# Twelve opening steps of a causal attention, issued among the units of the feed-forward before it

## The chip, the cores and the metric

The kernel runs on one core of a Trainium2 chip. The metric is the device time of one execution in microseconds (us). The engines are TensorE (PE for its matmuls, PEld for its weight loads), VectorE (DVE), ScalarE (ACT), GpSimd (POOL) and SyncE (SP, which here only issues DMAs).

## The reference

Two layers work on x of 8 images x 512 tokens x 256 features in fp32. Layer 0 is a full 16-head attention plus a mixture of 8 experts. Layer 1, to which the change belongs, adds two things to x, both computed from its layernorm `xn`:

```python
qkv = xn @ Wqkv_w.T + Wqkv_b                 # 16 heads of 16
ctx = causal_attn(q, k, v)                   # softmax of q.k / 4 under a causal mask
q2  = conv1d(ctx, conv_w, 3 taps) + conv_b   # new queries
ctx2 = causal_attn(q2, k, v)                 # the same keys and values
attn = ctx2 @ out_w.T + out_b
...
H   = gelu((xn @ U1) @ V1 + b1)              # rank 64, 1024 hidden
ffn = (H @ U2) @ V2 + b2
x   = x + attn + ffn
```

## The kernel before

Everything for one image (512 tokens) fits on the 128 partitions, features or tokens across. The order of instructions on every engine is the order in which the program issues them; each engine takes its own in that order, and waits on the others by semaphores.

**The feed-forward** of layer 1 is a loop over 32 pairs of hidden chunks: 8 images (`b`) x 4 pairs (`c2`). Its units: `ffn_in` (L981) multiplies an image by U1 and DVE copies the result to `pT` (L986); `ffn_hidden` (L993) makes two hidden chunks at once, each on 64 of the array's rows, and ACT takes the gelu (L999); `ffn_rank` (L1006) sums the two chunks over U2, on 64 columns each, into bank 7; `ffn_out` (L1018) first has DVE copy the rank-64 result to `fqT` (L1013), then multiplies by V2 in two halves, each added by DVE into `acc` (L1022). Pair `n` issues, in this order: `ffn_in` of the next image (if `c2` is 1), the pieces of `second` due there, the hidden chunks of pair `n + 1`, the rank of pair `n`, and `ffn_out` (if `c2` is 3). `second` carries out the list `THIRD` beside pairs 0 to 20: gathers of expert results (`g`), their sums (`+`, `P`, L525), statistics, norms (`n`, `N`, on ACT, L260), and the transposition of images 4 to 7 to features (`f`, L269: two halves, copied out by DVE, L271, and by ACT, L273).

**The banks.** PSUM has eight banks that one list of names shares out. `bank(kind)` hands out the banks of a kind in turn. In the feed-forward, `hidden` has banks 0 to 3, `mm` has 4 to 6 and bank 7 holds the rank's sum.

**Layer 1's attention** is a list of 64 jobs: first attentions (`key` 1) for 8 images x 4 groups of four heads, and the second ones (`key` 2) seven places behind them in the list. A job has six steps of maxima and, 12 steps later (`LEAD[1]`), six steps of exponentials. `run` counts steps `t` over all jobs: at step `t` it issues the maxima of job `t // 6` (`scores`, L348) and the exponentials of job `(t - 12) // 6` (`exps`, L397, a mask matmul, L415, and ACT's Exp, L424), with the matmuls of both interleaved; then one task from a list with due times (`todo1`); then the attention matmuls due (`attend`, L437, from five steps after a job's first exponentials). A maxima step is two heads, each on 32 of the array's rows, over 512, 128 + 384 or 256 keys, and DVE reduces each part (L368). So in steps 0 to 11 there are maxima alone. What the list gives to these steps: projections of queries and keys for jobs 0 and 1 ahead of step 0 (`project`, L296, taken out by DVE, L286, for queries and by ACT, L288, for keys); values of image 0 at steps 1 and 2 (L306, L314); the transposition of job 0's maxima at step 6 (`shift`, L378, copied by L381, and four DMAs, L385, that put them into a spare row of the queries); projections for jobs 2 and 3 at steps 7 and 8. The kind `mx` (maxima) has three banks there, `sc` (exponentials) three, `av` one, `mm` one.

**The pools.** The pool `l1` (mask, value buffer, exponentials `e`, the convolution's input `ctxT`, `cT`) and `q1` (queries, keys) are opened behind the feed-forward, when the pools `mid` (its weights) and `ffn` are closed. POOL's adds of the output biases to `acc` (L1164) are issued while the list of jobs is built, that is ahead of step 0, one for each image.

Of the kernel before, what the change touches and what calls it, by code (L numbers as in the profile page):

```python
# [152 lines left out]
def block_kernel(ctx: ExitStack, tc: tile.TileContext, x, a0_wqk, a0_bqk, a0_wv, a0_bv, cent, experts,  # L153
# [168 lines left out]
    class Job:  # L322
# [64 lines left out]
        def exps(self, i):  # L387
            blocks, pr = SC_SEQ[self.seq][i]
            heads = [bank("sc") for _ in range(2)]
            parts, at = [], 0  # L390
            for kc in blocks:
                lo = kc * P if self.causal else 0
                parts.append((kc, at, lo))
                at += S - lo
            mm = [
                [
                    lambda h=h, kc=kc, at=at, lo=lo: nc.tensor.matmul(  # L397
                        heads[h % 2][:, at : at + S - lo],
                        lhsT=self.k[h * PH : (h + 1) * PH, kc * P : (kc + 1) * P],
                        rhs=self.q[h * PH : (h + 1) * PH, lo:],  # L400
                        start=kc == blocks[-1],
                        stop=not self.causal,
                    )
                    for h in (2 * pr, 2 * pr + 1)
                ]
                for kc, at, lo in reversed(parts)
            ]
            n = at

            def after():  # L410
                if self.causal:


                    for h in range(2):
                        nc.tensor.matmul(  # L415
                            heads[h][:, : len(blocks) * P], lhsT=ident_bf, rhs=mask_t[:, : len(blocks) * P],
                            start=False, stop=True,
                        )
                e = self.pool.tile(
                    [P, 2, n], F32, tag=f"e{blocks[0]}" if self.causal else "e", name=f"e{self.nm}_{i}",  # L420
                    bufs=3 if self.causal else 4,
                )
# [20 lines left out]
                )  # L443

    def run(jobs, work_of, layer, per_step, most):
        steps, lead = STEPS[layer], LEAD[layer]
        end = steps * len(jobs)
        if layer == 1:
# [120 lines left out]
    with ExitStack() as l0:  # L569
# [347 lines left out]
        jobs = []  # L917
        for b in range(NB):
            for g in range(HG):
                job = Job(f"0_{b}_{g}", False, 1.0, vbuf[b % 2], g, l0_done, q0)  # L920
                job.b = b
                jobs.append(job)

# [50 lines left out]
    cb_sb = load([P, 2, 2], conv_b, "cb_sb")  # L974
    ow_sb = load([P, 2, D], out_w, "ow_sb")

    with tc.tile_pool(name="ffn", bufs=1, side="right", reuse_waits="tile") as ffn:
        def ffn_in(b):
            ps = bank()
            for k in range(2):  # L980
                nc.tensor.matmul(  # L981
                    ps, lhsT=u1_sb[:, k, :, :].rearrange("p i r -> p (i r)"), rhs=xT1[b][:, k, :],
                    start=(k == 0), stop=(k == 1),
                )
            pT = ffn.tile([P, S], F32, tag="pT", name=f"pT{b}", bufs=2)
            nc.vector.tensor_copy(pT, ps)  # L986
            return pT

        def ffn_hidden(b, c2, pT):
            ps = [bank("hidden") for _ in range(2)]  # L990
            for i in range(2):
                fc, r = 2 * c2 + i, slice(i * RANK, (i + 1) * RANK)
                nc.tensor.matmul(  # L993
                    ps[i], lhsT=v1_sb[r, fc * P : (fc + 1) * P], rhs=pT[r, :], start=True, stop=True
                )
            hT = ffn.tile([P, 2, S], F32, tag="hT", name=f"gT{b}_{c2}", bufs=3)
            for i in range(2):
                fc = 2 * c2 + i
                nc.scalar.activation(  # L999
                    hT[:, i, :], ps[i], AF.Gelu_apprx_tanh, bias=fb1_sb[:, fc : fc + 1]  # L1000
                )
            return hT

        def ffn_rank(pq, c2, hT):
            for i in range(2):
                nc.tensor.matmul(  # L1006
                    pq[i * RANK : (i + 1) * RANK, :], lhsT=u2_sb[:, 2 * c2 + i, :], rhs=hT[:, i, :],
                    start=(c2 == 0), stop=(c2 == NFC // 2 - 1),
                )

        def ffn_out(b, pq):
            qT = ffn.tile([P, S], F32, tag="qT", name=f"fqT{b}", bufs=2)
            nc.vector.tensor_copy(qT, pq)  # L1013
            for h in range(2):
                ps = bank()
                for j in range(2):
                    c = 2 * h + j
                    nc.tensor.matmul(  # L1018
                        ps[:, j * D : (j + 1) * D], lhsT=qT[:, c * P : (c + 1) * P], rhs=v2_sb, start=True, stop=True
                    )  # L1020
                a = acc[b][:, 2 * h : 2 * h + 2, :].rearrange("p c d -> p (c d)")
                nc.vector.tensor_tensor(a, a, ps, ALU.add)  # L1022

        share_banks(hidden=banks[:4], mm=banks[4:7])
        late = iter(THIRD)
        pTs = {0: ffn_in(0)}
        ahead = [(0, 0, ffn_hidden(0, 0, pTs[0]))]
        pairs = [(b, c2) for b in range(NB) for c2 in range(NFC // 2)]
        pq = None
        out_of = None  # L1030
        for n, (b, c2) in enumerate(pairs):
            if c2 == 1 and b + 1 < NB:
                pTs[b + 1] = ffn_in(b + 1)
            second(next(late, ""))
            if n + 1 < len(pairs):
                nb, nc2 = pairs[n + 1]
                ahead.append((nb, nc2, ffn_hidden(nb, nc2, pTs[nb])))
            _, _, hT = ahead.pop(0)
            if c2 == 0:
                pq = banks[7]  # L1040
            ffn_rank(pq, c2, hT)
            if c2 == NFC // 2 - 1:
                ffn_out(b, pq)
# [6 lines left out]
    for i in range(2):  # L1050
        t = l1.tile([P, 2, S + 2], F32, tag=f"ctxT{i}", name=f"ctxT{i}", bufs=1)
        nc.gpsimd.memset(t[:, :, 0:1], 0.0)
        nc.gpsimd.memset(t[:, :, S + 1 : S + 2], 0.0)
        ctxT.append(t)

    cmask = l1.tile([P, S], F32, name="cmask", bufs=1)
    nc.gpsimd.memset(cmask, 0.0)
# [59 lines left out]
    def l1_done(job, t):  # L1117
# [13 lines left out]
        cT = l1.tile([P, 2, S], F32, tag="cT", name=f"cT{b}", bufs=1)  # L1131
# [24 lines left out]
        for h in range(2):  # L1156
            todo1.add(t + 6, t + 12 + h, 1.75, lambda h=h: project_out(h))

    firsts, seconds, jobs = [], [], []
# [124 lines left out]
```

## Time and profile before

| | us |
|---|---|
| median of three timed runs | 2101.22 |
| lowest, highest | 2099.24, 2106.05 |
| the profiled execution | 2090.77 |
| its span, first to last instruction | 2089.0 |
| feed-forward, first matmul to last | 987.9 to 1102 |
| steps 0 to 11 | 1102 to 1140 |
| granted PE clock, mean over the span | 0.983 |

The rows of the profile give times in microseconds from the span's start. "x4" counts instructions: an fp32 matmul is two of them. A number in square brackets in the timeline is the time in which the engine had nothing to do before the row, with what ended it. "issue" is time in which an engine waited for nothing that the profile shows. The granted clock is a share of full speed.

### The profile page before, as it was taken

The numbers are of one execution on the slowest core, as the hardware profiler recorded it, in microseconds if no ns is written. First come the engines' busy times: TensorE is split into PE (matmuls) and PEld (weight loads), VectorE is DVE, ScalarE is ACT, GpSimd is POOL, SyncE is SP. The second block draws the span as 40 slices with busy tenths as digits, with TensorE's granted clock in tenths as the row PEclk, the third lists the DMA queues.
The fourth block names the chain that finished last, engine by engine and source line by source line (L and its number), as shares of the span: only waits on it lengthen the run. The fifth ranks groups of instructions, "written<-read, shape, count | busy, mean of one in ns | idle before, by whom it ended". The sixth has DMA issues, their size and how long they took to land.

```text
span 2089.0 us, 35592 instructions
## 1 busy us (share of the span) xinstructions
PE 2005.6 (96%) x13672; PEld 1019.1 (49%) x13672; DVE 1229.8 (59%) x3565; ACT 867.3 (42%) x1690; POOL 203.0 (10%) x245
## 2 busy tenths in 40 slices
PE   5899999999999999998898999999999999999998
PEld 3334555555555455542334455555555545554554
DVE  5765554555455554565425666666666666666763
ACT  4443333333333333336541444444444444444444
POOL 4361010010110100013310000000000000000000
PEclk8899999999999999999997999999999999999999
DMA  9025132222322223102000000000000000000000
GB/s 330 24 65 184 59 116 83 93 80 96 117 79 97 74 102 114 67 26 79 21 0 1 2 2 2 2 12 2 2 13 2 12 2 12 2 12 2 2 12 21
DMA packets 46057, 105.60 MB, mean 51 GB/s; under 512 B 5952, under 2 KB 33984, under 8 KB 42944
## 3 DMA queue, kind: packets, MB, share of 16 engines
q0 software_dynamic: 6384, 59.78, 7.7%
q1 hardware_dynamic: 38656, 42.62, 6.1%
q8 instruction: 107, 1.75, 0.4%
q10 hardware_dynamic: 848, 0.93, 0.1%
q14 instruction: 62, 0.51, 0.1%
HBM read 76.05 MB, written 26.48 MB: 49 GB/s over the span
## 4 chain that ended last, share of the span: by engine, by line
PE 88%; DVE 6%; ACT 2%; issue 2%; DMA 1%; SPq 0%; POOL 0%; ACTq 0%; DVEq 0%; POOLq 0%
PE bank L348 30%; PE bank L437 13%; PE bank L810 8%; PE bank L831 8%; PE bank L296 5%; PE bank L415 4%; PE bank L1088 4%; PE bank L397 3%; PE bank L306 3%; DVE m L365 2%; PE bank L1106 2%; PE bank L993 1%; PE bank L1140 1%; PE bank L269 1%; PE bank L1006 1%
## 5 line engine op out<-in xcount | busy, mean ns | idle before, releaser
L424 ACT ACTIVATE e<-bank 128x512 f32<-128x512 f32 (+1 forms) x1280 | 638.8, 552 | 923.0 <-PE bank L397 464.6
L348 PE MATMUL bank<-k,q 32*128 32x512 f32 (+3 forms) x3072 | 759.3, 534 | 22.3 <-DVE m L365 18.4
L397 PE MATMUL bank<-q,k 32*128 32x512 f32 (+3 forms) x3072 | 689.4, 533 | 4.2 <-DMA q<-mT 3.4
L368 DVE CUSTOM_DVE_ANT_0 jk<-bank,cmask 128x512 bf16<-128x512 f32 (+3 forms) x1024 | 502.8, 491 | 241.5 <-PE bank L348 162.2
L348 PEld LDWEIGHTS bank<-k,q 32*128 32x128 f32 x3072 | 301.1, 187 | 381.5 <-issue 158.6
L365 DVE TENSOR_REDUCE m<-bank 128x1 f32<-128x512 f32 x512 | 328.9, 685 | 142.6 <-PE bank L397 112.1
L437 PE MATMUL bank<-e,v 128*32 128x512 f32 (+3 forms) x3072 | 318.8, 503 | 0.0
L397 PEld LDWEIGHTS bank<-q,k 32*128 32x128 f32 x3072 | 272.0, 186 | 17.6 <-issue 9.9
L810 PE MATMUL bank<-hsT,w 128*128 128x256 f32 x736 | 179.7, 389 | 1.3 <-DVE hsT L793 1.3
L831 PE MATMUL bank<-w,hT 128*128 128x256 f32 x736 | 169.2, 383 | 0.0
L810 PEld LDWEIGHTS bank<-hsT,w 128*128 128x128 f32 x736 | 133.5, 190 | 69.7 <-issue 52.8
L831 PEld LDWEIGHTS bank<-w,hT 128*128 128x128 f32 x736 | 136.5, 190 | 37.3 <-issue 20.9
L437 PEld LDWEIGHTS bank<-e,v 128*32 128x32 f32 x3072 | 67.8, 109 | 137.3 <-issue 132.3
L415 PE MATMUL bank<-mask_t,ident_bf 128*128 128x128 bf16 (+1 forms) x768 | 123.6, 245 | 0.0
L415 PEld LDWEIGHTS <-ident_bf 128*128 128x128 bf16 x768 | 44.1, 98 | 155.4 <-issue 140.4
L823 DVE TENSOR_SCALAR hT<-bank,w 128x256 f32<-128x256 f32 x92 | 44.5, 484 | 110.4 <-ACT hT L821 110.4
L1088 PE MATMUL bank<-ctxT,cw_sb 128*128 128x256 f32 x384 | 90.0, 384 | 2.1 <-DVE q L286 1.8
L368 DVE DVE_READ_ACCUMULATOR2_ANT m<- 128x1 f32 x1024 | 84.9, 83 | 0.1
L840 DVE TENSOR_TENSOR f<-bank,w 128x256 f32<-128x256 f32 x46 | 19.5, 425 | 102.8 <-PE bank L831 102.8
L821 ACT ACTIVATE hT<-bank,w 128x256 f32<-128x256 f32 x92 | 43.6, 474 | 79.8 <-PE bank L810 79.8
L1088 PEld LDWEIGHTS bank<-ctxT,cw_sb 128*128 128x128 f32 x384 | 70.2, 190 | 13.1 <-DVE q L286 3.2
L288 ACT ACTIVATE k<-bank,bqk,rows 128x512 f32<-128x512 f32 x64 | 46.3, 773 | 69.8 <-PE bank L296 60.4
(187 smaller groups left out, 1409.7 us busy)
## 6 DMA issues: line engine op xcount, KB each, us to landing
hs_d<-zeros SPq DMA_DIRECT2D x2, 5888.0 KB
hs<-hs_d SPq DMA_DIRECT2D x46, 256.0 KB
q<-mT SPq DMA_DIRECT2D x384, 2.0 KB
fs_d<-f SPq DMA_DIRECT2D x23, 256.0 KB
acc<-in_x SPq DMA_DIRECT2D x8, 512.0 KB
out<-acc SPq DMA_DIRECT2D x8, 512.0 KB
cw_sb<-in_conv_w SPq DMA_DIRECT2D x1, 768.0 KB
wqk<-in_a_wqk ACTq DMA_DIRECT2D x1, 512.0 KB
```

The lines of the kernel that those rows point to most:

```text
L296: nc.tensor.matmul(ps, lhsT=w[:, k, col : col + P], rhs=src[:, k, :], start=(k == 0), stop=(k == 1))
L306: nc.tensor.matmul(ps[:, j * D : (j + 1) * D], lhsT=src[:, k, c * P : (c + 1) * P], rhs=w[:, k, :], start=(k == 0), stop=(k == 1),)
L348: lambda h=h, qc=qc, at=at, nk=nk: nc.tensor.matmul(heads[h % 2][:, at : at + nk], lhsT=self.q[h * PH : (h + 1) * PH, qc * P : (qc + 1) * ...
L365: nc.vector.tensor_reduce(self.m[:, qc, h, :], src, AX.X, ALU.max, negate=True)
L368: nc.vector.tensor_tensor_reduce(out=junk[:, :nk], in0=src, in1=cmask[:, S - nk :], scale=1.0, scalar=-3e38, op0=ALU.add, op1=ALU.max, acc ...
L397: lambda h=h, kc=kc, at=at, lo=lo: nc.tensor.matmul(heads[h % 2][:, at : at + S - lo], lhsT=self.k[h * PH : (h + 1) * PH, kc * P : (kc + 1 ...
L415: nc.tensor.matmul(heads[h][:, : len(blocks) * P], lhsT=ident_bf, rhs=mask_t[:, : len(blocks) * P], start=False, stop=True,)
L424: nc.scalar.activation(e[:, h, :], heads[h][:, :n], AF.Exp, scale=self.scale)
L437: nc.tensor.matmul(self.av[h * PH : (h + 1) * PH, lo:], lhsT=self.v[:, kc, 4 * self.g + h, :], rhs=es[h // 2][:, h % 2, :], start=first, s ...
L810: nc.tensor.matmul(ps[:, i * TB : (i + 1) * TB], lhsT=w[:, O_W1 + k * FF + fc * P : O_W1 + k * FF + (fc + 1) * P], rhs=self.hsT[:, k, :], ...
L831: nc.tensor.matmul(ps[:, 0:D], lhsT=self.hT[:, fc, j * P : (j + 1) * P], rhs=w[:, O_W2 + fc * D : O_W2 + (fc + 1) * D], start=(fc == 0), s ...
L1088: nc.tensor.matmul(ps[:, :w], lhsT=cw_sb[:, k, tap, c * P : (c + 1) * P], rhs=ctxT[b % 2][:, k, tap + lo : tap + lo + w], start=(k == 0 an ...
```

## The change

The function `run` becomes a generator that yields after every step. It is made ahead of the feed-forward, and the feed-forward's loop asks it for one step after pairs 8, 10, 12, ... 30, so that steps 0 to 11 are issued there; the rest of the steps follow behind the loop. For this, the pools `l1` and `q1` are opened before the feed-forward, and a new pool `e1` for what is only needed from step 12 on (exponentials, `ctxT`, `cT`) is opened after it. In the feed-forward the kind `mm` has bank 4 alone, and the maxima have banks 5 and 6. The mask and the third value buffer are filled ahead of the feed-forward, and POOL's adds of the output biases come behind it.

```diff
     def run(jobs, work_of, layer, per_step, most):
...
             work_of.fill(t, per_step, most)
             attend(t)
+            yield t
         work_of.drain()
...
-        run(jobs, todo, 0, MOE_PER_STEP, 99)
+        for _ in run(jobs, todo, 0, MOE_PER_STEP, 99):
+            pass
...
-    mids.close()
-    banks_causal()
     l1 = ctx.enter_context(tc.tile_pool(name="l1", bufs=2, reuse_waits="tile"))
     q1 = ctx.enter_context(tc.tile_pool(name="q1", bufs=5, reuse_waits="tile"))
...
     def l1_job(key, n):
         b, g = divmod(n, HG)
-        if key == 1 and g == 0:
-            nc.gpsimd.tensor_tensor(acc[b], acc[b], ob_sb.unsqueeze(1).to_broadcast([P, NC, D]), ALU.add)
-        job = Job(f"{key}_{b}_{g}", True, 0.25, vbuf[b % 3], g, l1_done, l1)
+        job = Job(f"{key}_{b}_{g}", True, 0.25, vbuf[b % 3], g, l1_done, ep)
...
-    run(jobs, todo1, 1, 99.0, 1)
+
+    steps = run(jobs, todo1, 1, 99.0, 1)
+    with tc.tile_pool(name="ffn", bufs=1, side="right", reuse_waits="tile") as ffn:
...
-        share_banks(hidden=banks[:4], mm=banks[4:7])
+        share_banks(hidden=banks[:4], mm=banks[4:5], mx=banks[5:7])
...
             if c2 == NFC // 2 - 1:
                 ffn_out(b, pq)
+            if n >= len(pairs) - 2 * LEAD[1] and n % 2 == 0:
+                next(steps)
+
+    mids.close()
+    ep.append(ctx.enter_context(tc.tile_pool(name="e1", bufs=3, reuse_waits="tile")))
+    for i in range(2):
+        t = ep[0].tile([P, 2, S + 2], F32, tag=f"ctxT{i}", name=f"ctxT{i}", bufs=1)
+        nc.gpsimd.memset(t[:, :, 0:1], 0.0)
+        nc.gpsimd.memset(t[:, :, S + 1 : S + 2], 0.0)
+        ctxT.append(t)
+    banks_causal()
+    for b in range(NB):
+        nc.gpsimd.tensor_tensor(acc[b], acc[b], ob_sb.unsqueeze(1).to_broadcast([P, NC, D]), ALU.add)
+    for _ in steps:
+        pass
```

The feed-forward's functions are otherwise as they were, moved below the list of jobs.

More of the change, by code (lines that the diff above doesn't have):

```diff
@@ L418, in after @@
                         )
-                e = self.pool.tile(
+                e = self.pool[-1].tile(
                     [P, 2, n], F32, tag=f"e{blocks[0]}" if self.causal else "e", name=f"e{self.nm}_{i}",
@@ L919, in block_kernel @@
             for g in range(HG):
-                job = Job(f"0_{b}_{g}", False, 1.0, vbuf[b % 2], g, l0_done, q0)
+                job = Job(f"0_{b}_{g}", False, 1.0, vbuf[b % 2], g, l0_done, [q0])
                 job.b = b
@@ L975, in block_kernel @@
     ow_sb = load([P, 2, D], out_w, "ow_sb")
[L977 to L1022, printed above, removed]
-        share_banks(hidden=banks[:4], mm=banks[4:7])
[L1025 to L1043, printed above, removed]
@@ L1049, in block_kernel @@
     ctxT = []
[L1050 to L1054, printed above, removed]
     cmask = l1.tile([P, S], F32, name="cmask", bufs=1)
@@ L1130, in l1_done @@
             return
-        cT = l1.tile([P, 2, S], F32, tag="cT", name=f"cT{b}", bufs=1)
+        cT = ep[0].tile([P, 2, S], F32, tag="cT", name=f"cT{b}", bufs=1)
         for k in range(2):
@@ L1157, in l1_done @@
             todo1.add(t + 6, t + 12 + h, 1.75, lambda h=h: project_out(h))
-    firsts, seconds, jobs = [], [], []
+    firsts, seconds, jobs, ep = [], [], [], []
     def l1_job(key, n):
         b, g = divmod(n, HG)
-        if key == 1 and g == 0:
-            nc.gpsimd.tensor_tensor(acc[b], acc[b], ob_sb.unsqueeze(1).to_broadcast([P, NC, D]), ALU.add)
-        job = Job(f"{key}_{b}_{g}", True, 0.25, vbuf[b % 3], g, l1_done, l1)
+        job = Job(f"{key}_{b}_{g}", True, 0.25, vbuf[b % 3], g, l1_done, ep)
         job.b, job.key = b, key
@@ L1194, in block_kernel, with ffn_in, ffn_hidden, ffn_rank @@
             l1_job(2, n - LAG)
-    run(jobs, todo1, 1, 99.0, 1)
+    steps = run(jobs, todo1, 1, 99.0, 1)
+    with tc.tile_pool(name="ffn", bufs=1, side="right", reuse_waits="tile") as ffn:
+        def ffn_in(b):
+            ps = bank()
+            for k in range(2):
+                nc.tensor.matmul(
+                    ps, lhsT=u1_sb[:, k, :, :].rearrange("p i r -> p (i r)"), rhs=xT1[b][:, k, :],
+                    start=(k == 0), stop=(k == 1),
+                )
+            pT = ffn.tile([P, S], F32, tag="pT", name=f"pT{b}", bufs=2)
+            nc.vector.tensor_copy(pT, ps)
+            return pT
+        def ffn_hidden(b, c2, pT):
+            ps = [bank("hidden") for _ in range(2)]
+            for i in range(2):
+                fc, r = 2 * c2 + i, slice(i * RANK, (i + 1) * RANK)
+                nc.tensor.matmul(
+                    ps[i], lhsT=v1_sb[r, fc * P : (fc + 1) * P], rhs=pT[r, :], start=True, stop=True
+                )
+            hT = ffn.tile([P, 2, S], F32, tag="hT", name=f"gT{b}_{c2}", bufs=3)
+            for i in range(2):
+                fc = 2 * c2 + i
+                nc.scalar.activation(
+                    hT[:, i, :], ps[i], AF.Gelu_apprx_tanh, bias=fb1_sb[:, fc : fc + 1]
+                )
+            return hT
+        def ffn_rank(pq, c2, hT):
+            for i in range(2):
+                nc.tensor.matmul(
+                    pq[i * RANK : (i + 1) * RANK, :], lhsT=u2_sb[:, 2 * c2 + i, :], rhs=hT[:, i, :],
+                    start=(c2 == 0), stop=(c2 == NFC // 2 - 1),
+                )
+        def ffn_out(b, pq):
+            qT = ffn.tile([P, S], F32, tag="qT", name=f"fqT{b}", bufs=2)
+            nc.vector.tensor_copy(qT, pq)
+            for h in range(2):
+                ps = bank()
+                for j in range(2):
+                    c = 2 * h + j
+                    nc.tensor.matmul(
+                        ps[:, j * D : (j + 1) * D], lhsT=qT[:, c * P : (c + 1) * P], rhs=v2_sb, start=True, stop=True
+                    )
+                a = acc[b][:, 2 * h : 2 * h + 2, :].rearrange("p c d -> p (c d)")
+                nc.vector.tensor_tensor(a, a, ps, ALU.add)
+        share_banks(hidden=banks[:4], mm=banks[4:5], mx=banks[5:7])
+        late = iter(THIRD)
+        pTs = {0: ffn_in(0)}
+        ahead = [(0, 0, ffn_hidden(0, 0, pTs[0]))]
+        pairs = [(b, c2) for b in range(NB) for c2 in range(NFC // 2)]
+        pq = None
+        out_of = None
+        for n, (b, c2) in enumerate(pairs):
+            if c2 == 1 and b + 1 < NB:
+                pTs[b + 1] = ffn_in(b + 1)
+            second(next(late, ""))
+            if n + 1 < len(pairs):
+                nb, nc2 = pairs[n + 1]
+                ahead.append((nb, nc2, ffn_hidden(nb, nc2, pTs[nb])))
+            _, _, hT = ahead.pop(0)
+            if c2 == 0:
+                pq = banks[7]
+            ffn_rank(pq, c2, hT)
+            if c2 == NFC // 2 - 1:
+                ffn_out(b, pq)
+            if n >= len(pairs) - 2 * LEAD[1] and n % 2 == 0:
+                next(steps)
@@ new lines, in block_kernel @@
+    mids.close()
+    ep.append(ctx.enter_context(tc.tile_pool(name="e1", bufs=3, reuse_waits="tile")))
+    for i in range(2):
+        t = ep[0].tile([P, 2, S + 2], F32, tag=f"ctxT{i}", name=f"ctxT{i}", bufs=1)
[7 more added lines that the diff above has]
+        pass
```

## The prediction

> **What bounds the kernel now.** I read the page first, then the chain of waits around the feed-forward, then windows by stage, then the timeline where a bank is reused. The page says TensorE (PE) is the bound, and that its clock is granted in full except around 1100 to 1150 us.
>
> ```profile
> PE 2005.6 (96%) x13672; PEld 1019.1 (49%) x13672; DVE 1229.8 (59%) x3565; ACT 867.3 (42%) x1690; POOL 203.0 (10%) x245
> ...
> PEclk8899999999999999999997999999999999999999
> ```
>
> The chain shows the feed-forward as almost pure PE work, and then the twelve steps.
>
> ```profile
> 1080.83 1.91 PE bank L981 x4
> 1082.74 1.06 PE bank L993 x4
> 1083.80 1.01 PE bank L1006 x4
> ...
> 1089.02 0.70 DVE fqT L1013
> 1089.72 0.04 issue
> 1089.77 2.00 PE bank L1018 x8
> ...
> 1118.10 1.11 PE bank L348 x4
> 1119.20 0.67 DVE jk L368
> ...
> 1133.20 1.98 PE bank L296 x4
> ```
>
> One pair of the feed-forward is hidden 1.06 plus rank 1.01; an image adds ffn_in 1.91 and ffn_out 0.74 (a DVE copy PE waits for) plus 2.00: 13.0 us, all PE. A step is 1.11 of maxima (0.56 for the 256-key ones), sometimes a projection (1.98) or values (1.98), with waits for DVE between.
>
> ```profile
> 1017.40:1102.10 84.70, 77.77 (x297) 29.37 (x298) 20.66 (x35) 41.77 (x69) 14.13 (x6) 1.00 0.00 0
> 1102.10:1140.10 38.00, 33.10 (x99) 15.56 (x97) 20.47 (x71) 4.17 (x5) 2.34 (x1) 0.80 0.00 1
> 1140.10:1158.10 18.00, 18.00 (x86) 9.24 (x85) 9.02 (x37) 5.66 (x12) 0.00 (x0) 0.50 0.01 2
> ...
> 1118.35:1121.76 3.41, 2.98 (x14) 1.24 (x10) 2.76 (x10) 0.00 (x0) 0.00 (x0) 1.00 0.00 0
> ...
> 1312.90:1316.31 3.41, 3.41 (x28) 2.21 (x28) 2.67 (x11) 2.12 (x4) 0.00 (x0) 1.00 0.02 5
> ```
>
> The columns are window, length, busy PE, PEld, DVE, ACT, POOL, then granted clock. The feed-forward from image 2 on (first row) keeps PE busy for 77.8 of 84.7 us: there is little room. The twelve steps (second row) take 38.0 us at a mean clock of 0.80, and steps 12 to 17 (third row) run wholly at half clock.
>
> **The clock, from the rows.** It changes on a grid of 3.41 us. I weigh PE's busy time by the share of the array's row strips in use: maxima alone use two of four. The window 1118.35 to 1121.76 has 2.98/2/3.41 = 0.44, and the next ones run at 0.50; windows at 0.41 (1108.11) and 0.44 (1135.41) did the same. Windows with a dense projection and a gap, 1.98/3.41 = 0.58 (1104.69), stayed at 1.00. So the edge lies between 0.44 and 0.58. Four strips at once at full clock keep it (the 1312.90 row); at half clock they did not win it back in six windows, until the first attention matmul (L437) at 1156.3.
>
> The Trainium skill, "TensorE: Matmul & The Clock Gate", section "Why this matters for your kernels", asks only that PE not idle for some 3 us between matmuls; by it alone nothing here would slow down, and no window of the changed feed-forward either. The 1118.35 row, busy for 2.98 of 3.41 us, differs, and I go by the row.
>
> **What is removed.** The 38.0 us between the end of ffn_out at 1102.05 and step 12 at 1140.05.
>
> **What the feed-forward gains.** Steps 0 to 11 follow pairs 8, 10, ... 30 on PE, in order. PE work: maxima 2 jobs x 2 x (1.11 + 1.11 + 0.56) = 11.1; four projections 7.9; two values 4.0; one transpose 0.3: 23.3 us. PE idles only 2.6 us there that this can fill, at images 2 and 3 (16.45 and 15.1 us against 13.0 plus 0.87 of transposes), where it waits for ACT's norms: -2.6.
>
> **The bank.** The feed-forward's other matmuls rotate over banks 4 to 6; now bank 4 alone serves them and the steps' tasks, as 5 and 6 hold maxima. Each reuse waits for the copy out. Its price is in these rows:
>
> ```profile
> 1089.77 2.00 PE L1018 MATMUL bank<-v_sb,fqT 128*128 128x256 f32 x8 [0.82 <-DVE fqT L1013]
> 1090.93 0.69 DVE L1022 TENSOR_TENSOR acc<-acc,bank 128x512 f32<-128x512 f32 x1 [1.22 <-PE bank L1018]
> ...
> 1105.55 1.98 PE L296 MATMUL bank<-yT,wqk 128*128 128x512 f32 x4 [1.62 <-DVE q L286]
> ```
>
> The first half of ffn_out ends at 1090.77, DVE's add ends at 1091.62, and PE follows 0.05 later: 0.90 us, in which everything behind it on PE waits too.
> - ffn_out's second half: 8 x 0.9 = 7.2.
> - The four transposed images (pairs 11, 14, 17, 20): second half after the first's copy, 4 x 0.9 = 3.6; and before the first half 0.9 to 1.0 after values (pair 11), ffn_in (17) and ffn_out (20): 2.9.
> - ffn_in after values (pair 13) 1.0, after the transposed maxima (pair 21; DVE has 1.55 of maxima queued first, then 0.27) 1.8, after a k projection (pair 25; ACT's two takes, 1.45) 1.65: 4.4.
> - Step 0: k's projection after q's 1.62, maxima after the first k take 0.92: 2.5, as before the change.
>
> Sum 20.6. The lower bound is step 0's 2.5 alone; I take 20.6, since each wait has its row and PE issues in order. The feed-forward grows by 23.3 - 2.6 + 20.6 = 41.3, against 38.0 removed: **+3.3**.
>
> The Trainium skill, "Perfetto Trace Analysis", section "Optimizing Tensor Performance", speaks against this edit: independent matmul groups should rotate through PSUM banks so that copying one out overlaps the next group's matmuls. By it the waits come in full, without it only step 0's remain, and the growth would be 23.2; the 1.62 us row sides with it.
>
> **The clock after.** Step 12 now follows dense pairs. Steps 12 to 17 at full clock are bound by DVE: three such steps take 5.0 us (its maxima rows run from 1312.53 to 1317.55), so 10.1 for six, 0.3 for a copied transpose, 1.0 for L437: 11.4, against 18.1 before (1140.05 to 1158.14); and 1.2 us more that ran at half clock shrink to 0.6: **-7.3**. Bounds: 0 if the clock falls anyway; -9.6 if DVE bounded nothing and all 19.3 us halved. But the waits thin some windows: at pair 21 half of 1.11, 0.3, then 1.8 of nothing and 0.35 of ffn_in is 1.2/3.41 = 0.35, below the edge for about two thirds of the grid's phases. At pair 20, 0.9 idle, 1.0, 0.9 idle, 0.44 and 0.17 idle make 1.44/3.41 = 0.42, and pairs 14 and 17 come to about the same, in a fifth of the phases each. One fallen window costs half of 3.41: **+1.7** (bounds 0 to 4 x 1.7).
>
> **Covered edits.** The eight POOL adds (2.35 us each, L1164) move from within the feed-forward to behind it, 19 us of POOL beside steps 12 on; acc is next needed by L1147 about 240 us later. The mask and value memsets (2.9 us) move ahead of the last gathers, where POOL idles 8.9 us; uncovered they cost 2.9. The moved transpose's four DMAs leave on SP some 45 us before step 12 reads them. DVE's maxima (1.0 to 2.15 us) stand ahead of fqT's copy, behind 2.07 us of PE: at most 0.1. ACT's Exp table load (1.28) falls under the last ffn_out (3.6). The e tiles' new pool waits only for ffn_out's own reads.
>
> **Sum:** 3.3 - 7.3 + 1.7 = -2.3 us. The profiled execution's 2090.8 (span 2089.0, 1.8 around it) becomes 2088.5; it lies 10.4 below the median of the timed runs, 2101.2, which goes to 2098.9. Its own range, with no to three fallen windows and 5 us either way on the waits, is 2092 to 2106.
>
> **Rivals.**
> - *The waits cost half.* PEld loads the next weights during a wait, and some waits may meet ones already there (ACT's norms at images 2 and 3, the 0.74 before ffn_out). Growth 23.3 - 2.6 + 10.3 = 31.0; -38.0 - 7.3 gives -14, 2087. For it: PE has hidden work on other banks queued close behind. Against: it is queued behind, not ahead.
> - *The clock is lost at the seam (slower).* If a window near the last ffn_out (0.74 and 0.9 idle of 3.6) or of steps 12 to 14, DVE-bound, falls under the edge, it stays at half until L437, since four strips did not lift it in six windows. Then -7.3 is gone, and with three fallen windows (5.1): 3.3 + 5.1 = +8.4, 2110. It decides once that share is below 0.44 to 0.58. Against: the 1312.90 row.
> - *Neither clock nor wait differs much*: the stretch merely changes place, within 2 us.
>
> **How the numbers follow.** The forecast has 0.52, the cheap waits 0.26, the lost clock 0.20, the last 0.02. A measurement of this kernel tells about 0.3% (6.3 us) from no change. The forecast's fast quarter (no window falls, waits over-counted by 2.3 us or more) is beyond that: 0.15. Faster 0.15 + 0.26 = 0.41; same 0.37 + 0.02 = 0.39; slower 0.20. The range runs from a cheap-waits case to near the lost clock: 2086 to 2109.
>
> **What would show it.** Right: step 12 near 1145 (1102.05 + 41.3 + 1.7); L1018 waiting 0.9 for L1022 eight times; clock 1.00 in the 12 us behind it; L437 some 11 us after step 12. Wrong: growth under 33 us (waits oversized), or clock 0.50 behind step 12 (the seam), or fallen windows in most images.

## The result, and the profile after

The changed kernel is slower. Beside the kernel before on one chip, its median is 2108.2 us against 2098.7 (13 runs each): a ratio of 1.0046, 95% interval 1.0029 to 1.0063. Timed twice more beside other kernels, it came to 1.0069 (1.0041 to 1.0098) and 1.0050 (1.0035 to 1.0065). The forecast was 2.3 us less than before; the medians say 9.5, 12.7 and 9.6 more. The first of these, 2108.2 us, still lies at the upper end of the stated range of 2086 to 2109, but the change went the other way than forecast.

The page of the profiled execution (2110.55 us, span 2108.8) answers to the two lines shown of before:

```profile
PE 2010.1 (95%) x13672; PEld 1012.8 (48%) x13672; DVE 1230.6 (58%) x3565; ACT 867.6 (41%) x1690; POOL 202.8 (10%) x245
...
PEclk9999999999999999998999899999999999999999
```

PE's busy time is 4.5 us more than before, and the row of the clock looks no worse: the 7 of before, at 1097 to 1149 us, has become an 8 at 949 to 1002 and one at 1160 to 1213 us. The span is nevertheless 19.8 us longer, so the place has to be looked for. 10.9 of these lie ahead of the change: the first hidden matmul starts at 1001.50 us, where the profile of before has 990.61. The same start came at 991.8 and 999.0 in two more profiles of the same changed kernel, so this part belongs to the execution. What can be compared is the stretch from that first hidden matmul to the end of the first attention matmuls (L437): 167.6 us before; 175.5, 181.9 and 174.1 in three profiles of the changed kernel, 9.6 more in the mean, as much as the medians differ (9.5 to 12.7). Of the kernel before there is only this one profile.

The windows by stage, of the changed kernel (length, busy PE, PEld, DVE, ACT, POOL, granted clock): feed-forward with its twelve steps, step 12 to the end of the first L437, and two neighbouring clock windows within the latter.

```profile
1001.50:1159.65 158.15, 130.56 (x477) 47.12 (x477) 58.97 (x158) 57.33 (x92) 16.52 (x19) 0.98 0.03 7
1159.65:1177.03 17.38, 16.38 (x90) 7.24 (x89) 8.87 (x34) 6.94 (x13) 12.24 (x6) 0.69 0.01 2
1162.73:1166.14 3.41, 2.41 (x21) 1.41 (x20) 1.10 (x6) 2.40 (x5) 3.41 (x2) 1.00 0.01 2
1166.14:1169.56 3.42, 3.42 (x16) 1.10 (x11) 1.81 (x9) 0.84 (x3) 3.42 (x3) 0.50 0.02 5
```

The first row: 158.15 us, of which PE idles 27.6. Before, the feed-forward took 111.44 us with 9.8 idle, so it grew by 46.7, not by 43.0 (41.3 and 1.7 for the clock). The second row: behind step 12 the mean clock is 0.69, and the stretch takes 17.4 us where 11.4 was forecast and 18.2 stood before. The last two rows show where the clock goes: a window in which PE is busy for 2.41 us, and half clock behind it.

The waits of PE, by what ended them (us in total, times, longest), for the first of these stretches:

```profile
PE bank L1164 <- DVE acc L1168: 6.6, 8, 0.9
PE bank L1164 <- DVE fqT L1159: 5.8, 7, 0.9
PE bank L269 <- DVE yT L271: 3.1, 4, 0.8
PE bank L296 <- DVE q L286: 1.7, 1, 1.7
PE bank L1127 <- DVE mT L381: 1.6, 1, 1.6
PE bank L1127 <- ACT k L288: 1.5, 1, 1.5
```

These are the waits for bank 4 as they were priced: ffn_out's second half (L1164) for DVE's add of the first, eight times; the second transposed half (L269) for the copy of the first, four times; ffn_in (L1127) behind the transposed maxima 1.6 us and behind a projection 1.5.

The timeline at the seam, where step 12 starts at 1159.65:

```profile
1156.68 1.13 PE L1164 MATMUL bank<-v_sb,fqT 128*128 128x256 f32 x4 [0.82 <-DVE fqT L1159]
1157.85 0.69 DVE L1168 TENSOR_TENSOR acc<-acc,bank 128x512 f32<-128x512 f32 x1 [1.22 <-PE bank L1164]
1158.60 1.13 PE L1164 MATMUL bank<-v_sb,fqT 128*128 128x256 f32 x4 [0.78 <-DVE acc L1168]
...
1159.76 0.69 DVE L1168 TENSOR_TENSOR acc<-acc,bank 128x512 f32<-128x512 f32 x1 [1.22 <-PE bank L1164]
...
1161.56 0.28 PE L415 MATMUL bank<-mask_t,ident_bf 128*128 128x128 bf16 x2
...
1161.86 1.28 ACT L424 ACT_TABLE_LOAD   x1 [7.29 <-issue]
...
1163.15 1.08 ACT L424 ACTIVATE e<-bank 128x512 f32<-128x512 f32 x2
...
1163.81 0.58 PE L397 MATMUL bank<-q,k 32*128 32x384 f32 x1 [1.00 <-ACT e L424]
```

ffn_out's halves take 1.13 us each, split by a wait, where both together took 2.00 before. And ACT's load of the Exp table, which the prediction put under ffn_out, starts only at 1161.86, though ACT had nothing to do for 7.29 us: 0.02 us behind the mask matmul (L415) that completes the Exp's own operand, and 1.4 us behind the end of ffn_out's last add. The first exponentials are 1.28 us late for it, PE waits 1.00 us for their bank, and the clock falls to half behind this window. In the profile of before the same load stood beside the maxima, 6.4 us ahead of the first exponentials:

```profile
1136.69 1.28 ACT L424 ACT_TABLE_LOAD   x1
1143.11 1.08 ACT L424 ACTIVATE e<-bank 128x512 f32<-128x512 f32 x2 [5.14 <-PE bank L415]
```

### The profile page after: what moved, and what is told of

Same layout as the page of the kernel before. It is cut to its first block, busy times and chain, and to the rows that moved or that the text cites. A ratio compares the mean times of both kernels' runs of the same rounds, so it can differ in the third digit from the quotient of the medians.

```text
span 2108.8 us, 35586 instructions
## 1 busy us (share of the span) xinstructions
PE 2010.1 (95%) x13672; PEld 1012.8 (48%) x13672; DVE 1230.6 (58%) x3565; ACT 867.6 (41%) x1690; POOL 202.8 (10%) x245
## 5 line engine op out<-in xcount | busy, mean ns | idle before, releaser
L437 PE MATMUL bank<-e,v 128*32 128x512 f32 (+3 forms) x3072 | 320.8, 505 | 0.0
L397 PEld LDWEIGHTS bank<-q,k 32*128 32x128 f32 x3072 | 271.3, 186 | 21.4 <-issue 10.5
L437 PEld LDWEIGHTS bank<-e,v 128*32 128x32 f32 x3072 | 67.7, 109 | 139.5 <-issue 134.5
L415 PE MATMUL bank<-mask_t,ident_bf 128*128 128x128 bf16 (+1 forms) x768 | 123.2, 244 | 0.0
L415 PEld LDWEIGHTS <-ident_bf 128*128 128x128 bf16 x768 | 43.9, 97 | 155.0 <-issue 139.7
L1145 ACT ACTIVATE gT<-bank,fb_sb 128x512 f32<-128x512 f32 x64 | 40.3, 683 | 68.8 <-PE bank L1139 64.0
```

The source lines that it names most:

```text
L397: lambda h=h, kc=kc, at=at, lo=lo: nc.tensor.matmul(heads[h % 2][:, at : at + S - lo], lhsT=self.k[h * PH : (h + 1) * PH, kc * P : (kc + 1 ...
L415: nc.tensor.matmul(heads[h][:, : len(blocks) * P], lhsT=ident_bf, rhs=mask_t[:, : len(blocks) * P], start=False, stop=True,)
L437: nc.tensor.matmul(self.av[h * PH : (h + 1) * PH, lo:], lhsT=self.v[:, kc, 4 * self.g + h, :], rhs=es[h // 2][:, h % 2, :], start=first, s ...
```

## The experiments

The theory after this: the waits for bank 4 cost as priced and somewhat more, and the clock behind step 12 is lost because the late table load thins one window. The rivals: the clock falls there whatever the table does; the waits only change places; POOL's adds behind the feed-forward slow the steps.

The table puts the stretches of all profiles together (us; "idle" is PE idle in the feed-forward with its steps, "half" the number of 3.41 us windows that ran at half clock in it; a dash where the idle time was not worked out; a stretch at half clock that starts just ahead of step 12 is not counted). For before and for one bank alone, the twelve steps stand behind the feed-forward and are counted with it.

| kernel | first hidden to step 12 | idle | half | step 12 to end of first L437 | ratio to before (95%) |
|---|---|---|---|---|---|
| before | 149.4 | 14.7 | 4 | 18.2 | 1 |
| changed | 158.2 | 27.6 | 2 | 17.4 | 1.0046 (1.0029 to 1.0063) |
| changed, again | 164.2 | 27.6 | 6 | 17.7 | 1.0069 (1.0041 to 1.0098) |
| changed, third | 156.5 | 27.6 | 1 | 17.6 | 1.0050 (1.0035 to 1.0065) |
| early Exp | 156.5 | 27.5 | 1 | 12.5 | 1.0036 (1.0018 to 1.0054) |
| early Exp, again | 158.1 | – | 2 | 16.0 | 1.0027 (1.0011 to 1.0043) |
| shared banks | 133.0 | 9.9 | 0 | 16.4 | 0.9917 (0.9900 to 0.9935) |
| shared banks, early Exp | 133.0 | 9.9 | 0 | 11.7 | 0.9882 (0.9864 to 0.9900) |
| shared banks, own memory for the first e | 133.0 | – | 0 | 11.7 | 0.9894 (0.9877 to 0.9912) |
| the same as early Exp with shared banks, ffn_out later | 128.1 | 4.9 | 0 | 11.6 | 0.9868 (0.9844 to 0.9893) |
| one bank, rest as before | 170.9 | 28.1 | 7 | 17.4 | 1.0097 (1.0080 to 1.0113) |
| changed, adds back | 156.8 | – | 1 | 17.6 | 1.0060 (1.0033 to 1.0086) |
| changed, two long fillers | 156.5 | – | 1 | 17.9 | 1.0043 (1.0024 to 1.0061) |
| changed, fillers behind | 158.1 | 27.5 | 2 | 15.9 | 1.0044 (1.0026 to 1.0062) |
| before, fillers | 149.1 | – | 0 | 20.1 | 1.0029 (1.0011 to 1.0047) |

**The Exp table loaded early.**

```diff
+            if n + 2 == len(pairs):
+                hint = small.tile([P, 1], F32, tag="hint", name="hint", bufs=1)
+                nc.scalar.activation(hint, fb1_sb[:, 0:1], AF.Exp)
```

> One Exp of 128x1 follows the last gelu on ACT, so that the table is loaded under pair 31's matmuls and not at step 12. Seam theory: the 1.00 us in which PE waits for L424 at step 12 is gone, the window behind it is no longer thin, the granted clock stays 1.00 up to the first L437, and step 12 to the end of that L437 takes 11 to 12 us where the changed kernel takes 17.4: 5 to 6 us less than the changed kernel. Rival, thin windows at the seam whatever the table does (two waits of 0.8 for ffn_out's copies stand just ahead, and the steps wait for DVE): the clock falls to 0.50 all the same, and the time changes by 0 to -1.3 us.

The load ran straight behind the last gelu (1142.38), the wait of 1.00 us was gone, the clock stayed at 1.00, and step 12 to the end of the first L437 took 12.5 us. So far the theory was right. The ratio, 1.0036, only leans below the changed kernel's; so it was run again, beside the changed kernel.

> The changed kernel, timed beside the early Exp on one chip. Half clock behind step 12 as before; two to six windows at half clock in the feed-forward; 9 to 14 us above the kernel before.

> The early Exp once more, beside the changed kernel. By the profiles it saves 5 us behind step 12 and nothing in the feed-forward, whose waits and half-clock windows stay: the median 3 to 7 us under the changed kernel's. Rival, what the seam gains is lost elsewhere: the same median within 2 us.

The medians were 2105.97 and 2107.57 us, 1.6 apart: less than expected, and the intervals of the two ratios overlap. The changed kernel had one window at half clock in its feed-forward, where two to six were expected. In the second profile of the early Exp the table was early too, and yet the clock fell, one window later:

```profile
1160.63:1164.04 3.41, 3.34 (x27) 1.63 (x20) 2.17 (x10) 1.96 (x5) 3.41 (x2) 1.00 0.01 2
1164.04:1167.46 3.42, 3.42 (x17) 1.57 (x19) 1.83 (x6) 1.08 (x3) 3.42 (x3) 0.50 0.02 5
```

PE was busy for 3.34 of 3.41 us, almost all of it with matmuls on 32 rows, those of maxima and exponentials together (four short mask matmuls use 128). The prediction had read from the 1312.90 row that four strips at once keep full clock; here they did not. Weighed by strips as there, this window comes to about 0.62 (an estimate from its matmul rows), above the predicted edge of 0.58. The same program held the clock once and lost it once, so it seems that the place of the grid decides whether such a window is cut out of steps 12 to 14; with the late load there was one in all three profiles of the changed kernel, with the early load in one of two.

**Maxima and the rest share banks 4 to 6, without and with the early Exp.**

```diff
-        share_banks(hidden=banks[:4], mm=banks[4:5], mx=banks[5:7])
+        share_banks(hidden=banks[:4], mm=banks[4:7])
+        rings["mx"] = rings["mm"]
```

> Maxima and the other matmuls of the feed-forward take turns on banks 4, 5 and 6 together; no other edit. Bank theory: the waits for bank 4 go, 8 x 0.8 at ffn_out's second half, 4 x 0.85 and 3 x 0.85 at the transposed images, 4 of about 1.2 at ffn_in, together some 16 us of the 31.8 us that PE idles in the changed kernel's feed-forward, and with them the two windows at half clock (3.4): 15 to 19 us less than the changed kernel. The stretch behind step 12 stays at half clock, since the table load stays where it is. Rival, the waits only change their place (a shared bank waits for DVE's maxima in its turn): 0 to -6 us.

> The early Exp and the shared banks together. If the two causes are separate, their gains add: 20 to 25 us less than the changed kernel, 10 to 15 less than the kernel before. If the clock behind step 12 hangs on the waits in the last ffn_out as much as on the table, it holds here though it may not with the early Exp alone.

Windows by stage of shared banks alone, then with the early Exp:

```profile
991.80:1124.82 133.02, 123.08 (x479) 47.37 (x480) 58.66 (x158) 57.38 (x92) 15.49 (x19) 1.00 0.03 9
1124.82:1141.24 16.42, 15.86 (x90) 6.92 (x89) 8.87 (x34) 6.94 (x13) 13.28 (x6) 0.70 0.01 2
```

```profile
990.41:1123.42 133.01, 123.08 (x479) 47.35 (x479) 58.67 (x158) 58.87 (x94) 15.48 (x19) 1.00 0.03 9
1123.42:1135.07 11.65, 11.58 (x90) 5.80 (x89) 8.81 (x34) 5.66 (x12) 11.65 (x6) 1.00 0.01 3
```

With one edit of two lines the feed-forward falls from 158.15 to 133.0 us, more than the 15 to 19 expected (the 31.8 us of idle time in that expectation is too high; the first row after the change gives 27.6). 17.7 of the 25.1 is idle time. The other 7.5 is PE's busy time (130.56 to 123.08): 3.3 for the two windows at half clock (1.63 each, the difference of busy time between the profiles with two and one), and 4.2 that the prediction had not priced, of which 8 x 0.26 = 2.1 are ffn_out's split halves. The early Exp is then worth 7.6 us on one chip (2074.68 to 2067.10), 4.8 of them in the second row, where the clock goes from 0.70 to 1.00. With both edits the kernel is 24.3 us below the one before, where 10 to 15 was expected. Both kernels are faster than before: the twelve steps are worth moving, with banks to move them into.

**One bank, and nothing else of the change.**

```diff
-        share_banks(hidden=banks[:4], mm=banks[4:7])
+        share_banks(hidden=banks[:4], mm=banks[4:5])
```

> The kernel before, with bank 4 alone for the feed-forward's matmuls other than hidden and rank; the twelve steps stay behind it with their banks as they were. Bank theory, as the prediction priced it: 8 x 0.9 at ffn_out's second half, 4 x 0.9 at the second halves of the transposes and 2 to 3 before their first halves: 13 us more than the kernel before, up to 18 with three windows fallen to half clock. Rival, the single bank costs only where the steps use it too: under 5 us more.

The feed-forward took 132.9 us in place of 111.44. Its idle time rose by 13.4 (9.8 to 23.2), close to the 13 that the prediction's prices give without the steps; 11.6 of it are waits for bank 4. The rest, 8.1, is busy time: 11.8 us of half clock in that stretch cost up to 5.9, and the split halves 2.1. The median rose by 21.1 us, more than the 18 expected. The bank alone is dearer than the whole change.

**POOL's adds back in the feed-forward.**

```diff
+            nc.gpsimd.tensor_tensor(acc[b], acc[b], ob_sb.unsqueeze(1).to_broadcast([P, NC, D]), ALU.add)
...
-    for b in range(NB):
-        nc.gpsimd.tensor_tensor(acc[b], acc[b], ob_sb.unsqueeze(1).to_broadcast([P, NC, D]), ALU.add)
```

> The changed kernel itself, timed beside the next three. Seam theory: half clock from some 6 us behind step 12 to the first L437, two windows at half clock within the feed-forward, some 10 us above the kernel before. Rival, the first comparison owed part of its 9.6 us to layer 0, whose end came 10.9 us later in that one profiled execution: with layer 0's end near 991 us the kernel is less than 5 us above the kernel before.

> The changed kernel with each image's POOL add of the output bias back behind its ffn_out, inside the feed-forward. If the eight adds (18.5 us of POOL beside steps 12 on) cost nothing where they are, as the prediction had it, the time is the changed kernel's within 2 us. Rival, they slow DVE's maxima or the stores of the exponentials behind step 12: step 12 to the end of the first L437 falls below 17.4 by 2 us or more.

Behind step 12 nothing moved: 17.6 us against 17.7. The medians, 2099.85 and 2104.47 us, are 4.6 apart, more than the 2 expected, but the runs of the one spread over 13 us and of the other over 18, and the ratios, 1.0060 and 1.0069 on the same chip, have overlapping intervals. So the profile shows no cost of the adds where they are, and the times can't tell 5 us. The changed kernel itself started its feed-forward at 991.8 us here, was 12.7 us over the kernel before all the same, and had six windows at half clock, where two were expected.

**ffn_out one pair later.** The copy of `fqT` is issued behind the rank, the matmuls of `ffn_out` behind the next hidden matmuls.

```diff
+            if out_of is not None:
+                ffn_out(*out_of)
+                out_of = None
             _, _, hT = ahead.pop(0)
...
-                ffn_out(b, pq)
+                out_of = (b, qT)
```

> Early Exp, shared banks, and each image's ffn_out put one pair later, behind the next hidden matmuls (1.06 us), so that DVE's copy of fqT runs under them. If what is left of the feed-forward's waits is that copy, seven of the eight waits of 0.82 go, each with some 0.13 us of restart: 6 to 7 us less than the early Exp with shared banks, so about 1.5% below the kernel before. Rival, the wait moves on to rank, whose gelus then come late: no change.

Seven of the eight waits went: idle time from 9.9 to 4.9 us, the feed-forward from 133.0 to 128.1, the ratio 0.9868 (2061.76 us against 2091.78). The restarts that had been counted on top didn't show: busy time stayed at 123.2. This is the fastest version by its ratio, 1.3% under the kernel before (1.5% was expected); its interval overlaps that of early Exp with shared banks, so the gain over that version rests on the profile.

**Is it the thin window?** Three kernels fill windows with matmuls whose results nobody reads. The first puts two of them into PE's wait at step 13.

```diff
+                        if layer == 1 and t == lead + 1 and n == 0 and h == 1 and i == 1:
+                            for _ in range(2):
+                                nc.tensor.matmul(
+                                    banks[6], lhsT=ident, rhs=xT1[0][:, 0, :], start=True, stop=True
+                                )
```

> The changed kernel, its table load left where it is, with two matmuls of 128x128 by 512 that nobody reads (about 0.5 us each, into bank 6, which is free there) in the place at step 13 where PE waits 1.00 us for ACT. If the clock is lost because that window uses too little of the array, it now uses about twice as much, the clock stays 1.00 up to the first L437, and step 12 to the end of that L437 takes about 13 us in place of 17.4: 4 to 5 us less than the changed kernel, though it computes more. Rival, the late table load itself costs the time: no gain, or 1 us more.

A miss: step 12 to the end of the first L437 took 17.9 us, not 13. One such matmul takes 0.99 us, not 0.5, so that the two overran the wait. The filled window kept its clock, and the next one lost it:

```profile
1147.76:1151.17 3.41, 3.41 (x21) 1.34 (x20) 0.86 (x3) 2.37 (x3) 3.41 (x3) 1.00 0.01 2
1151.17:1154.58 3.41, 3.34 (x24) 1.74 (x22) 2.30 (x11) 1.74 (x4) 3.41 (x2) 1.00 0.02 5
1154.58:1157.99 3.41, 3.41 (x19) 1.28 (x19) 1.70 (x6) 1.08 (x2) 3.38 (x2) 0.50 0.00 0
```

The second has one in the wait and a shorter one in each of steps 14 to 17; the third has nothing of the change, and a short one in each of steps 0 to 17.

```diff
+                        if layer == 1 and t == lead + 1 and (n, h, i) == (0, 1, 1):
+                            nc.tensor.matmul(banks[6], lhsT=ident, rhs=xT1[0][:, 0, :], start=True, stop=True)
                         f()
+                if layer == 1 and lead + 1 < t < lead + 6 and n == 0:
+                    nc.tensor.matmul(
+                        banks[6][:, : S // 2], lhsT=ident, rhs=xT1[0][:, 0, : S // 2], start=True, stop=True
+                    )
```

> The changed kernel with its table load left late, with one matmul of 128x128 by 512 that nobody reads (0.99 us by the run before) in PE's wait of 1.00 us at step 13, and one of 128x128 by 256 (0.5 us) in each of steps 14 to 17, which wait for DVE. The array is then used to over half in every window behind step 12. Theory of the thin window: the granted clock stays 1.00 from step 12 to the first L437, which ends 12.5 to 14 us behind step 12 (17.4 in the changed kernel, 17.9 with the two long fillers alone): 3.5 to 5 us less than the changed kernel. Rival, the late table load takes the clock or the time in another way: half clock as before, and the fillers (3 us at full clock, 6 at half) make it 2 to 6 us slower than the changed kernel.

> The kernel before, with one matmul of 128x128 by 256 that nobody reads (0.5 us at full clock) in each of steps 0 to 17, beside its maxima. Nothing of the change is in it. Theory of the thin window: the three stretches at half clock among the twelve steps and behind them (3.4, 10.2 and 20.5 us in the profile) are gone; steps 12 to the end of the first L437 go from 17.4 to 12 to 14 us, and the twelve steps, which wait for DVE, change by -3 to +3: 3 to 8 us less than the kernel before, though it computes more. Rival, the clock falls for the waits and not for the little use of the array (PE still waits for DVE and for the copies of projections): the clock falls as before and the fillers add 9 us at full and up to 18 at half clock, less what the waits cover: 3 to 12 us more.

Windows by stage of the changed kernel with fillers behind step 12, and of the kernel before with fillers (twelve steps, then step 12 to the end of the first L437):

```profile
1149.02:1164.96 15.94, 15.92 (x100) 7.20 (x99) 8.87 (x34) 6.94 (x13) 12.23 (x6) 1.00 0.01 2
```

```profile
1104.12:1142.31 38.19, 34.17 (x127) 16.47 (x128) 21.50 (x74) 4.18 (x5) 2.34 (x1) 0.99 0.00 1
1142.31:1162.43 20.12, 20.10 (x101) 9.39 (x99) 8.55 (x35) 5.66 (x12) 0.00 (x0) 0.68 0.01 2
```

Fillers held the clock: at 1.00 behind step 12 with the table load still late, and at 0.99 through the twelve steps of the kernel before, which had 0.80, though PE idled there almost as long (4.0 us against 4.9). So more use of the array within a window holds the clock, and the late load acts by thinning a window. What share a window needs stays open: at the seam of the second kernel a window still fell, with fillers in it (PE busy for 2.85 us of 1138.25 to 1141.66), and the next four ran at half clock. In time the fillers gave nothing. In the first kernel their own work ate the gain (15.9 us, where 12.5 to 14 was expected; its ratio lies within the changed kernel's intervals). The second came out slower than the kernel before (1.0029; 2095.44 us against 2089.6), where 3 to 8 us less was expected: the twelve steps took 38.2 us as before, since the other matmuls fell from 33.3 to 28.2 us and the fillers added 8.4, and the stretch behind them took 20.1 us against 18.2.

**Why the load came late.** In the compiled program of before, the load waits for nothing and the first Exp behind it for PE alone. In the changed program the load itself waits for DVE and PE, and the Exp for an ACT instruction. The first tile of exponentials now lies in memory that `pT` and gelus of the last image used, so that the Exp has three engines to wait for, and two of these waits stand ahead of its load. The one on DVE is for the copy to `pT`, long done. The one on PE is for the mask matmul (L415), the Exp's own operand, and it is the one that ends late: the profile has ACT in this wait for 8.47 us, and the load starts 0.02 us behind L415. The last experiment gives this one tile memory that is free all the while (shared banks, no early Exp).

```diff
+    ep.append(ctx.enter_context(tc.tile_pool(name="e0", bufs=1, reuse_waits="tile")))
...
-                e = self.pool[-1].tile(
+                first = self.causal and self is jobs[0] and i == 0
+                e = self.pool[0 if first else -1].tile(
```

> Shared banks as before, no early Exp, but the first tile of exponentials (4 KB of a partition) lies in memory that is free all the while, not in what the feed-forward's last matmuls and adds still read and write. If that reuse is what held the table load back (ACT waited for DVE and PE ahead of the load), the load runs straight behind the last gelu, some 6 us before step 12's exponentials, the clock behind step 12 stays at 1.00, and the time is that of early Exp with shared banks: 1.1 to 1.2% below the kernel before, 7 us below shared banks alone. Rival, the load always comes with the first Exp's operands: idle of some 5 us ahead of it, half clock behind step 12, and 0.8% below the kernel before as with shared banks alone.

```profile
1127.70 1.27 ACT L1147 ACTIVATE gT<-bank,fb_sb 128x512 f32<-128x512 f32 x2 [0.80 <-PE bank L1141]
1128.98 1.28 ACT L425 ACT_TABLE_LOAD   x1
1134.34 1.09 ACT L425 ACTIVATE e<-bank 128x512 f32<-128x512 f32 x2 [4.08 <-PE bank L415]
```

The load runs straight behind the last gelu, the clock stays at 1.00, and the stretch takes 11.65 us, as with the early Exp. The ratio, 0.9894, lies between that of shared banks alone and that with the early Exp; the intervals overlap, so here the profile decides and not the time. By the ratios it is some 5 us below shared banks alone, where 7 was expected.

## Why the prediction was wrong

**The step that failed** is one of the covered edits: "ACT's Exp table load (1.28) falls under the last ffn_out (3.6). The e tiles' new pool waits only for ffn_out's own reads." It took the load to run as soon as ACT is free, and put no wait ahead of it. The load stood behind the waits of its Exp instead, and the wait that ended last was for the Exp's own mask matmul: the load started at 1161.86, not under ffn_out. By these rows a wait for ffn_out alone would have cost nothing: the last add ended at 1160.45, and 1.28 us later the mask matmul was still running (to 1161.84). Giving the tile other memory moved the load, which shows that the reuse of memory put the wait ahead of it. With that, the term **-7.3**, 6.7 of it for the stretch from step 12 to the end of the first L437, came to -0.6 there (18.2 to 17.6 in the mean of three profiles). Its size was right: where the clock held, the stretch took 11.65 to 12.5 us for a forecast of 11.4. The rival "the clock is lost at the seam", given 0.20 and +8.4, is what happened, but the late load is not among the reasons it names. Nor is the load the only way to lose the clock there, since it fell in one of two profiles with the early load and the bank alone.

**The waits for bank 4 were right, their price too low.** PE's idle time in the feed-forward grew by 17.8 us (9.8 to 27.6), where 20.6 - 2.6 = 18.0 was forecast. Of the 20.6, 18.1 were for new waits, and their rows add up to 16.3; shared banks took away 17.7, with step 0's 1.7 among it. The -2.6 is a slip: its own figures give 2.6 for image 2 and 1.2 for image 3, and of the 2.4 us that PE waited for ACT's norms before, 0.7 were left. What had no term is PE's longer busy time around the waits, 4.2 us. The 0.90 for a split ffn_out left out that two halves of 1.13 take longer than 2.00, which makes 2.1 of it; for the other 2.1 us the runs show no place. The rival that the waits cost half, given 0.26, has nothing left for it. The Trainium skill, "Perfetto Trace Analysis", section "Optimizing Tensor Performance", which spoke against this edit, was right: with three banks to rotate through, the feed-forward with the same steps took 25.1 us less.

**Fallen windows: 1.7 us forecast; two, six and one windows measured**, at 1.55 to 1.63 us each by PE's busy time, so 4.8 us in the mean. The pair 21 was named and fell in two of the three. What I left out are the windows around an ordinary ffn_out, with 0.82 to 0.89 and 0.78 to 0.85 us of idle close together. Two of them, each with the window behind it, in the second profile of the changed kernel:

```profile
1048.51:1051.92 3.41, 1.67 (x7) 0.90 (x6) 1.38 (x2) 0.03 (x1) 0.00 (x0) 1.00 0.00 0
1051.92:1055.34 3.42, 3.42 (x8) 1.29 (x7) 0.69 (x1) 0.00 (x0) 0.00 (x0) 0.50 0.00 0
1072.40:1075.82 3.42, 1.81 (x7) 1.31 (x8) 1.38 (x2) 1.26 (x3) 0.00 (x0) 1.00 0.00 0
1075.82:1079.23 3.41, 3.41 (x19) 1.23 (x17) 0.69 (x1) 1.81 (x4) 0.00 (x0) 1.00 0.01 2
```

Busy for 1.67 us, a window of dense matmuls lost the clock; busy for 1.81, it kept it (and another with 1.81, at 1137.26, lost it). That is a share of 0.49 to 0.53, within the predicted 0.44 to 0.58, and ffn_outs of the changed kernel stand on that edge. It is not sharp: a window with two projections at 1036.44 in the first profile kept the clock with 1.73 us. A window that falls also shifts all that follows against the grid, which is probably why the same program had one, two and six of them; no run tests that. The Trainium skill, "TensorE: Matmul & The Clock Gate", section "A second HAM failure mode: psum-queue depth-cycling", tells of such a swing of the clock in another kernel, from short waits between groups of matmuls, and this trace agrees: no wait in these windows is longer than 1.7 us.

**The sum, redone** with the mean of the three profiles: -2.3 forecast; the steps' work and the waits that shared banks leave -1.6 (the feed-forward of shared banks grew by 21.6, where 23.3 - 2.6 + 2.5 was forecast); bank waits -0.4; busy time around them +4.2; windows +3.1; the seam +6.7. That is +9.7, against +9.6 in the profiles and +9.5 to +12.7 in the medians.

**Right:** PE's work of the twelve steps within 2 us (shared banks made PE busy for 21.4 us more, where 23.3 was forecast), the added waits in place and number, POOL's adds at nothing that the profile shows, the size of steps 12 to 17 at full clock. Of the signs named, three spoke against the forecast: step 12 came at +46.7 and not by +43, the clock fell to 0.50 behind it, and L437 ended 17.4 us after step 12 began.

## What to carry to other kernels

A covered operation needs two things: an engine that is free, and no wait ahead of it. Follow a table load to the instruction it belongs to, and look at all that one waits for, its own operands and the memory of closed pools included: in this program reused memory put the wait for the operand ahead of the load. Before work is moved into a dense stretch, count the banks that are left there for it: two lines that let both kinds rotate over the same three banks turned +0.5% into -0.8%, an early Exp into -1.2%, and a copy put under other matmuls into -1.3%. Short waits are dearest where several fall into one clock window.

## What was not expected of the hardware

- A busy PE can lose its clock: busy for 3.34 of 3.41 us, nearly all with matmuls on 32 rows, it went to 0.50 (twice, above). With dense matmuls one window busy for 1.81 us kept it, and another lost it.
- Unread matmuls hold the clock: 0.80 became 0.99 in the twelve steps of the kernel before, at no gain, since their own 8.4 us of PE took up what the clock gave.
- The table load is no longer where it comes late: 1.28 us in all profiles. In the changed kernel the Exp follows 0.01 us behind it. What the load waits for came with the instruction that it serves: with one wait to its Exp the load had none (before, and with the tile in free memory), with three it had two.
